# Reordering the steps of the first layer's context attention and feed-forward: probability transposes later, down products in halves, normalizations emitted later

## The chip, the cores and the metric

One core of a Trainium2 chip runs the whole kernel. The metric is the device time in microseconds; lower is better. The time before is the median of 3 runs, 3416.09 us (3408.83 to 3417.53).

Engine names in the profile: PE is TensorE (PEld its weight loads), DVE is VectorE, ACT is ScalarE, POOL is GpSimd, SP is SyncE, which issues DMAs. Each engine works through its own queue in the order in which the program was built.

## The reference, cut to what matters

Two decoder layers on x of shape (8, 512, 256), with layer normalization after each of three sublayers. The change touches the second and third sublayer of the first layer:

```python
x = _layernorm(x + _L0_attn_ref(x, ...))
x = _layernorm(x + _L0_xattn_ref(x, ctx, ctx, mask))   # 16 heads of 16, 64 context keys, no projections
x = _layernorm(x + _L0_ffn_ref(x, ...))                # 256 -> 1024, gelu, 1024 -> 256, biases
x = _layernorm(x + _L1_attn_ref(x, ...))
...
```

`_L0_xattn_ref` masks and scales `q k^T`, takes a softmax over 64 keys and multiplies with the values. In `_L0_ffn_ref` the butterfly stages were folded into the two weight matrices earlier in the kernel.

## The kernel before, in words

The kernel runs stage after stage: the first layer's self-attention, then the stage of this change (context attention and feed-forward of layer 0, in one interleaved loop), then layer 1. x stays on chip as eight tiles `xs[b]`, one per batch element ("batch" below), each as 4 blocks of 128 rows.

The loop of the stage is near line 895: `for n in range(len(steps_) + 3)`, with `b, i = n // 4, n % 4`. A step is one block of 128 rows of one batch. PE is scheduled by hand here (`tc.manual_schedule(engines={PE})`): its queue has exactly the order of the calls. The queues of DVE, ACT and POOL are ordered by the scheduler of the language when the program is built, and fixed from then on; a call given to `tc.keep_in_program_order` is held to its place in the text.

The pieces of a step, in the order of before:

- `l0x_keys` (at i=0, line 699), for the next batch: two products on POOL that spread the context over heads (`bd`, L703), the mask's DMA (L710), and its bias on DVE (L712).
- `l0x_scores` (line 715): score matmuls into two PSUM tiles (`s_xs`, L725); DVE adds the mask bias and so empties PSUM (L735), takes the maximum (L741); POOL subtracts it (L742); ACT takes the exponential (L743); DVE sums (L744). The result `p` is used one step later.
- `l0x_transposes` (line 747) of the step before: PE turns the probabilities (`tP`, L755), ACT copies them to `pt` (L756).
- one piece `up` of the feed-forward (line 818): eight passes of 512 columns into `s_h` (L823), two gelus on ACT (L832). Exponential and gelu need different ACT tables, so each step loads two.
- `l0x_values` at i=0 (line 758): value products `s_xpv` (L764) from `pt`; ACT copies them to `oT` (L773); DMAs of a later batch's context values on SP (L780).
- `l0x_back` at i=1 (line 785): PE turns `oT` back (`tO`, L800), DVE divides by the sums (L802), POOL adds the residual (L808), `normed` follows.
- at i=2, `turned_x` of the next batch: PE turns x (`tT`, L695), ACT copies it to `xT` (L696).
- one piece `down` (line 834): 8 matmuls of one row block (`o_out`, L846). After two blocks DVE adds `xb`, which is x plus biases, made on POOL (L837), into `r` (L856); after the fourth, `normed`.
- at i=2, `ffn(b - 1)` (line 813): turns the normalized x once more and queues four `up` pieces and four `down` pieces.

`normed` (line 206): DVE statistics (L213, L214), plus epsilon (L215); POOL's power (`rs`, L216); DVE's shift (L220); then four scalings on ACT (L224) that write `xs[b]`. With `then` given, the last part (from L220) is not emitted but appended to a list.

The feed-forward lags: `ffn(b - 1)` is called at step i=2 of batch b, its `up` pieces run in the next four steps, its `down` pieces in the four after those. While a `down` list is empty, `one` takes a piece from `early` instead: the unfinished output of the self-attention and four transposes of the second matrix (`wdn_piece`).

PSUM: two buffers for `s` tiles (`s_xs` twice, `s_h`, and `s_xpv` share them), three banks for `t` tiles (`tP`, `tO`, `tT`, and the second half of a `down` result), one for `o` (its first half). A tile's buffer is written again once its last reader is done.

Of the kernel before, what the change touches and what calls it, by code (L numbers as in the profile page):

```python
# [11 lines left out]
F32 = mybir.dt.float32  # L12
I32 = mybir.dt.int32
AF = mybir.ActivationFunctionType
ALU = mybir.AluOpType
# [3 lines left out]
P = 128  # L19
S = 512  # L20
D = 256
S2 = 64
NT = S // P
# [26 lines left out]
def decoder_kernel(ctx: ExitStack, tc: tile.TileContext, a: dict, out: bass.AP):  # L50
    nc = tc.nc
    NB = a["x"].shape[0]
# [10 lines left out]
    pe, act, dve, pool, sp = nc.tensor, nc.scalar, nc.vector, nc.gpsimd, nc.sync  # L63
# [3 lines left out]
    work = ctx.enter_context(tc.tile_pool(name="work", bufs=2))  # L67
# [49 lines left out]
    one = const.tile([1, 1], F32, name="one")  # L117
# [11 lines left out]
    xs = [const.tile([P, NT, D], F32, name=f"x{b}") for b in range(NB)]  # L129
# [47 lines left out]
    dnb = const.tile([P, D], F32, name="dnb")  # L177
# [28 lines left out]
    def normed(dst, r, on_act=False, then=None):  # L206

        st = work.tile([P, NT, 6], F32, tag="st", name="st")
        mv = work.tile([P, NT, 2], F32, tag="mv", name="mv")
        ve = work.tile([P, NT], F32, tag="ve", name="ve")  # L210
        rs = work.tile([P, NT], F32, tag="rs", name="rs")
        for i in range(NT):
            dve.bn_stats(st[:, i, :], r[:, i, :])  # L213
            dve.bn_aggr(mv[:, i, :], st[:, i, :])  # L214
        dve.tensor_scalar(ve, mv[:, :, 1], LN_EPS, None, ALU.add)  # L215
        pool.tensor_tensor(rs, ve, mhalf, ALU.pow)  # L216

        def scaling(held=lambda instruction: instruction):
            if on_act:
                dve.scalar_tensor_tensor(ve, mv[:, :, 0], -1.0, rs, ALU.mult, ALU.mult)  # L220
            for i in range(NT):
                if on_act:
                    held(
                        act.activation(dst[:, i, :], r[:, i, :], AF.Identity, bias=ve[:, i : i + 1], scale=rs[:, i : i + 1])  # L224
                    )
                    continue
                dve.tensor_scalar(
                    dst[:, i, :], r[:, i, :], mv[:, i, 0:1], rs[:, i : i + 1], ALU.subtract, ALU.mult
                )

        if then is None:
            scaling()
        else:
            then.append(scaling)

    def r_tile():
        return work.tile([P, NT, D], F32, tag="r", name="r", bufs=1)
# [547 lines left out]
    def l0x_back(b):  # L785

        oT, sums = live.pop(("oT", b)), live.pop(("sums", b))
        rsum = ph.tile([P, NT, 16], F32, tag="rsum16", name="rsum16")
        for i in range(NT):
            dve.reciprocal(  # L790
                rsum[:, i, :].rearrange("p (c r e) -> p c r e", c=KC, r=4),
                sums[:, i, :].rearrange("p (r c e) -> p c r e", c=KC, r=4),
            )
        rx = ph.tile([P, NT, D], F32, tag="rx", name="rx", bufs=1)
        for i2 in range(2):
            t = t_tile("tO")
            for j in range(2):
                i = 2 * i2 + j
                for c in range(KC):
                    pe.transpose(t[:, 2 * j + c, :], oT[:, c, i * P : (i + 1) * P], ident)  # L800
            two = slice(2 * i2, 2 * i2 + 2)
            dve.tensor_tensor(  # L802
                rx[:, two, :].rearrange("p i (h n) -> p (i h) n", n=16),
                t.rearrange("p i (h n) -> p (i h) n", n=16),
                rsum[:, two, :].rearrange("p i h -> p (i h)").unsqueeze(2).to_broadcast([P, 32, 16]),
                ALU.mult,
            )
            pool.tensor_tensor(rx[:, two, :], rx[:, two, :], xs[b][:, two, :], ALU.add)  # L808
        normed(xs[b], rx, on_act=True)

    ups, downs = [], []

    def ffn(b):
        xT = turned_x(b)
        gs = gates[b % 2]
        made = {}

        def up(f2):
            s = s_tile("s_h")
            for j in range(2):  # L820
                f = 2 * f2 + j
                for c in range(KC):
                    pe.matmul(  # L823
                        s[:, j, :],
                        lhsT=wup[:, c, f * P : (f + 1) * P],
                        rhs=xT[:, c, :],
                        start=(c == 0),
                        stop=(c == KC - 1),
                    )
            for j in range(2):  # L830
                f = 2 * f2 + j
                act.activation(gs[f], s[:, j, :], AF.Gelu, bias=upb[:, f : f + 1])  # L832

        def down(i):
            if i == 0:
                xb = work.tile([P, NT, D], F32, tag="att", name="xb")
                pool.tensor_tensor(xb, xs[b], dnb.unsqueeze(1).to_broadcast([P, NT, D]), ALU.add)  # L837
                made["xb"], made["r"] = xb, r_tile()
            xb, r = made["xb"], made["r"]
            i2, j = i // 2, i % 2  # L840
            if j == 0:
                made["o"] = (t_tile("o_out").rearrange("p i n -> p (i n)") if i2 else o_tile("o_out")).rearrange(
                    "p (i n) -> p i n", i=2
                )
            for f in range(8):
                pe.matmul(  # L846
                    made["o"][:, j, :],
                    lhsT=gs[f][:, i * P : (i + 1) * P],
                    rhs=wdn[:, f, :],
                    start=(f == 0),  # L850
                    stop=(f == 7),
                )
            if j == 0:
                return
            two = slice(2 * i2, 2 * i2 + 2)
            dve.tensor_tensor(r[:, two, :], made["o"], xb[:, two, :], ALU.add)  # L856
            if i2 == 1:
                normed(xs[b], r, on_act=True)

        ups.extend(partial(up, f2) for f2 in range(4))  # L860
        waiting.append([partial(down, i) for i in range(NT)])

    waiting = []

    with phase("l0_context_ffn") as ph, tc.manual_schedule(engines={PE}):
        v2 = [ph.tile([P, 8, 32], F32, name=f"v2{n}", bufs=1) for n in range(2)]
        for n in range(2):
            pool.memset(v2[n], 0.0)
            l0x_context(n)
        l0x_keys(0)  # L870
        live["xT", 0] = turned_x(0)
        more = [slot(f"gate{n}") for n in range(2)]
        few = ph.tile([P, 8, S], F32, name="few", bufs=1)
        gates = [
            [few[:, f, :] for f in range(8)],
            [more[f // 4][:, f % 4 * S : (f % 4 + 1) * S] for f in range(8)],
        ]
        weights_of_layer_1()
        wdn = ph.tile([P, 8, D], F32, tag="wdn", name="wdn", bufs=1)

        def wdn_piece(f):
            t = t_tile("tW")
            for j in range(4):
                pe.transpose(t[:, j, :], wdnT[:, j % 2, (f + j // 2) * P : (f + j // 2 + 1) * P], ident)
            act.copy(wdn[:, f : f + 2, :].rearrange("p f n -> p (f n)"), t.rearrange("p j n -> p (j n)"))

        steps_ = [(b, i) for b in range(NB) for i in range(NT)]
        early = unfinished + [partial(wdn_piece, f) for f in range(0, 8, 2)]

        def one(queue):  # L890
            if queue:
                queue.pop(0)()
            elif early:
                early.pop(0)()

        for n in range(len(steps_) + 3):
            b, i = n // NT, n % NT
            if i == 0 and b + 1 < NB:
                l0x_keys(b + 1)
            if n < len(steps_):  # L900
                l0x_scores(b, i)
            if 0 < n <= len(steps_):
                l0x_transposes(*steps_[n - 1])
            one(ups)
            if i == 0 and b:
                l0x_values(b - 1)
            if i == 1 and b:
                l0x_back(b - 1)
            if i == 2 and b + 1 < NB:
                live["xT", b + 1] = turned_x(b + 1)  # L910
            if i == 3 and waiting and len(waiting) > 1 or (i == 3 and waiting and not ups):
                downs.extend(waiting.pop(0))
            one(downs)
            if i == 2 and b:
                ffn(b - 1)
        while ups or downs or waiting:
            if ups:
                ups.pop(0)()
            if not downs and waiting and (len(waiting) > 1 or not ups):
                downs.extend(waiting.pop(0))  # L920
            if downs:
                downs.pop(0)()

    turned = slot("turned").rearrange("p (two j n) -> p two j n", two=2, j=2)
    woT1 = slot("woT1").rearrange("p (c n) -> p c n", c=8)
# [808 lines left out]
```

## Time and profile before

| | us |
|---|---|
| median of the 3 runs | 3416.09 |
| lowest, highest | 3408.83, 3417.53 |
| the profiled execution, own time | 3412.61 |
| its span, first to last instruction | 3410.9 |
| mean granted TensorE clock | 0.974 |
| stage of the change: first `s_xs` to the next layer | 778.8 to 1184.4 |
| first `s_xs` of steps 7, 11, 15, 19, 23, 27, 31 (i=3) | 826.09, 866.21, 908.29, 957.43, 1005.91, 1055.73, 1102.94 |

Busy time of PE in the span is 3217.6 us. The page has one digit per 85 us; a row of digits shows tenths of busy time. In a line of the timeline the columns are start, duration (both us), engine, line, operation, output<-input, shape, count, and in brackets the idle time of that engine just before, with what ended it. A line of waits names who waited for what, then total us, times, and the longest.

### The profile page before, as it was taken

How to read it: one execution, taken by the hardware profiler on the slowest of the kernel's cores; microseconds unless marked ns; L12 is line 12 of the kernel's file. 1: busy time of each engine (PE TensorE's matmuls, PEld its weight loads, DVE VectorE, ACT ScalarE, POOL GpSimd, SP SyncE). 2: the span in 40 equal slices, each digit the busy share in tenths (PEclk: the TensorE clock that was granted, in tenths of full speed). 3: DMA queues.
4: the chain of work that ended last, by engine and by line, in shares of the span. 5: the costliest groups of instructions: out<-in, count | busy, mean ns of one | idle time of the engine just before them, and what ended most of it. 6: DMA issues, size and time to landing. Idle time of an engine off the chain costs nothing. (4 is left out here: it accounts for less than half of the span.)

```text
span 3410.9 us, 53375 instructions
## 1 busy us (share of the span) xinstructions
PE 3217.6 (94%) x19638; PEld 2030.8 (60%) x19638; DVE 1992.7 (58%) x6491; ACT 1590.2 (47%) x3280; POOL 1122.8 (33%) x1049
## 2 busy tenths in 40 slices
PE   7999999997888989999999999999999999999995
PEld 3444444445555656766666665555555557888884
DVE  5777777765455277787777865666776664100102
ACT  2444454455666355565556653444444443222222
POOL 3777777764333122222222210011111111222222
PEclk8999999998999999999999999999999999999997
DMA  4000011110000099323333320000000006666674
GB/s 138 26 26 29 29 32 44 40 52 12 18 2 1 27 254 240 44 38 38 41 40 43 42 44 4 10 14 23 20 20 18 14 18 205 186 187 185 186 231 136
DMA packets 166006, 235.00 MB, mean 69 GB/s; under 512 B 26569, under 2 KB 128649, under 8 KB 165746
## 3 DMA queue, kind: packets, MB, share of 16 engines
q1 hardware_dynamic: 139010, 175.83, 16.3%
q0 software_dynamic: 25584, 51.57, 10.7%
q10 hardware_dynamic: 1152, 4.19, 0.3%
q8 instruction: 155, 2.54, 0.3%
q14 instruction: 105, 0.86, 0.1%
HBM read 135.83 MB, written 61.11 MB: 58 GB/s over the span
## 5 line engine op out<-in xcount | busy, mean ns | idle before, releaser
L438 DVE CUSTOM_DVE_ANT_0 scored<-s_sc,decay 128x512 f32<-128x512 f32 x512 | 332.5, 687 | 191.0 <-PE s_sc L433 191.0
L290 ACT ACTIVATE p<-p,nm 128x384 f32<-128x384 f32 (+3 forms) x512 | 282.4, 552 | 256.0 <-DVE nm L279 256.0
L979 POOL DMA_DIRECT2D qk<-turned x256 | 203.7, 1222 | 579.2 <-PE s_sc L1019 300.0
L496 ACT ACTIVATE pt<-s_st 128x1024 f32<-128x1024 f32 x256 | 261.8, 1024 | 268.5 <-PE s_st L492 242.1
L1004 DVE TENSOR_SCALAR p<-p,rsum 128x576 f32<-128x576 f32 (+4 forms) x768 | 300.8, 434 | 10.2
L1223 ACT ACTIVATE p<-s_sc,nm 128x576 f32<-128x576 f32 x256 | 189.4, 742 | 195.5 <-DVE nm L1222 173.8
L1590 DVE TENSOR_SCALAR y<-o_y,share 128x256 f32<-128x256 f32 x71 | 34.3, 484 | 403.5 <-PE o_y L1570 403.5
L1553 PE MATMUL s_h<-xnT,we 128*128 128x256 f32 (+1 forms) x1248 | 258.8, 361 | 0.0
L1570 PE MATMUL o_y<-we,h 128*128 128x256 f32 x1136 | 251.4, 379 | 0.0
L279 DVE CUSTOM_DVE_ANT_0 p<-s_sc,tabs 128x384 f32<-128x384 f32 (+3 forms) x512 | 225.1, 484 | 44.7 <-PE s_sc L1019 42.4
L1591 POOL DMA_INDIRECT total<-y,to x71 | 110.2, 1552 | 385.9 <-DVE y L1590 198.7
L1570 PEld LDWEIGHTS o_y<-we,h 128*128 128x128 f32 x1136 | 215.3, 190 | 29.0
L1553 PEld LDWEIGHTS s_h<-xnT,we 128*128 128x128 f32 x1248 | 215.4, 190 | 23.9 <-ACT xnT L1532 0.2
L1222 DVE TENSOR_REDUCE nm<-s_sc 128x1 f32<-128x576 f32 x256 | 183.3, 749 | 77.2 <-PE s_sc L1218 76.1
L1052 ACT COPY pt<-tP 128x384 f32<-128x384 f32 (+1 forms) x384 | 167.0, 527 | 56.2 <-PE tP L1051 56.0
L1019 PE MATMUL s_sc<-qk 64*128 64x384 f32 (+3 forms) x1024 | 178.6, 462 | 14.7 <-DMA qk<-turned 9.5
L1051 PEld LDWEIGHTS tP<-ident,p 128*128 128x128 f32 x1280 | 141.3, 141 | 51.7 <-issue 30.5
L1218 PE MATMUL s_sc<-k,q 64*128 64x288 f32 x1024 | 166.3, 437 | 3.3 <-ACT p L1223 3.1
L1051 PE MATMUL tP<-ident,p 128*128 128x128 f32 x1280 | 163.1, 278 | 3.2 <-ACT pt L1052 2.2
L433 PE MATMUL s_sc<-k,q 32*128 32x512 f32 x1024 | 154.5, 647 | 3.2 <-ACT k L418 1.7
L450 DVE TENSOR_SCALAR_CACHE_REDUCE diag<-scored,mx 128x128 f32<-128x128 f32 x512 | 155.7, 342 | 0.0
L1074 PE MATMUL o_pv<-pt,vc 128*64 128x128 f32 (+1 forms) x2304 | 154.5, 288 | 0.0
(290 smaller groups left out, 6322.7 us busy)
## 6 DMA issues: line engine op xcount, KB each, us to landing
we<-in_mo_w SPq DMA_DIRECT2D x78, 1024.0 KB
rows_in<-zero SPq DMA_DIRECT2D x64, 530.0 KB
qk<-turned POOLq DMA_DIRECT2D x256, 128.0 KB, 4.6
coef<-in_ff_upw SPq DMA_DIRECT2D x40, 256.0 KB
coef<-in_ff_dnw SPq DMA_DIRECT2D x40, 256.0 KB
xr<-rows_in SPq DMA_DIRECT2D x32, 265.0 KB
x<-in_x SPq DMA_DIRECT2D x8, 512.0 KB
total<-x SPq DMA_DIRECT2D x8, 512.0 KB
```

Of the source, the lines that this page charges most:

```text
L279: dve.tensor_tensor_reduce(out=p[:, j, 0:n], in0=s[:, j, 0:n], in1=m, scale=-scale, scalar=3.0e38, op0=ALU.add, op1=ALU.min, accum_out=nm[ ...
L290: act.activation(p[:, j, 0:n], p[:, j, 0:n], AF.Exp, bias=nm[:, j : j + 1], scale=-1.0, accum_out=sums[:, at + j : at + j + 1],)
L438: dve.tensor_tensor_reduce(out=scored[:, h, :], in0=s[:, j, :], in1=decay[:, i, :], scale=1.0, scalar=-3.0e38, op0=ALU.mult, op1=ALU.max, ...
L496: tc.keep_in_program_order(act.activation(pt, s, AF.Exp, scale=1.0 / 16.0))
L979: pool.dma_start(out=qk[h : h + 32], in_=other[g : g + 32], accum_op=ALU.add)
L1004: dve.tensor_scalar(p[:, j, 0:n], p[:, j, 0:n], rsum[:, j : j + 1], None, ALU.mult)
L1019: pe.matmul(s[:, j, at : at + n], lhsT=q[h : h + 64, i * P : (i + 1) * P], rhs=k[h : h + 64, 0:n], start=True, stop=True,)
L1051: pe.transpose(t[:, n, :], p[:, j, at * P : (at + 1) * P], ident)
L1222: dve.tensor_reduce(nm[:, j : j + 1], s, AX.XY, ALU.max, negate=True)
L1223: act.activation(p[:, j, :].rearrange("p (t n) -> p t n", t=2), s, AF.Exp, bias=nm[:, j : j + 1], accum_out=sums[:, j : j + 1])
L1553: pe.matmul(s[:, j, :], lhsT=w1[:, c, f * P : (f + 1) * P], rhs=xnT[:, c, :], start=(c == 0), stop=(c == KC - 1),)
L1570: pe.matmul(o, lhsT=h[:, f, i * P : (i + 1) * P], rhs=w2[:, f, :], start=(f == 0), stop=(f == 7),)
```

## The change

The order of PE's calls in a step becomes: scores; half a `down` piece; `up`; the scaling part of a finished feed-forward normalization, if any; transposes of the step before; then by i the values, the way back, or the scaling part of the context normalization and `turned_x`; keys of the next batch (at i=0, now after the values); another half `down` piece; `ffn`. A `down` list has eight pieces of 4 matmuls in place of four of 8. The two scaling parts are held in program order. POOL's residual add moves to DVE. `xb` is made in `ffn`, not with the first `down` piece.

```diff
-            pool.tensor_tensor(rx[:, two, :], rx[:, two, :], xs[b][:, two, :], ALU.add)
-        normed(xs[b], rx, on_act=True)
+            dve.tensor_tensor(rx[:, two, :], rx[:, two, :], xs[b][:, two, :], ALU.add)
+        normed(xs[b], rx, on_act=True, then=backs)
...
-    ups, downs = [], []
+    ups, downs, backs, ends = [], [], [], []
...
         made = {}
+        xb = work.tile([P, NT, D], F32, tag="att", name="xb")
+        pool.tensor_tensor(xb, xs[b], dnb.unsqueeze(1).to_broadcast([P, NT, D]), ALU.add)
...
-        def down(i):
-            if i == 0:
-                xb = work.tile([P, NT, D], F32, tag="att", name="xb")
-                pool.tensor_tensor(xb, xs[b], dnb.unsqueeze(1).to_broadcast([P, NT, D]), ALU.add)
-                made["xb"], made["r"] = xb, r_tile()
-            xb, r = made["xb"], made["r"]
+        def down(n):
+            if n == 0:
+                made["r"] = r_tile()
+            r = made["r"]
+            i, half = n // 2, n % 2
             i2, j = i // 2, i % 2
-            if j == 0:
+            if j == 0 and half == 0:
...
-            for f in range(8):
+            for f in range(4 * half, 4 * half + 4):
...
-            if j == 0:
+            if j == 0 or half == 0:
                 return
...
-                normed(xs[b], r, on_act=True)
+                normed(xs[b], r, on_act=True, then=ends)
...
-        waiting.append([partial(down, i) for i in range(NT)])
+        waiting.append([partial(down, n) for n in range(2 * NT)])
...
+        def scale(queue):
+            if queue:
+                queue.pop(0)(tc.keep_in_program_order)
+
         for n in range(len(steps_) + 3):
             b, i = n // NT, n % NT
-            if i == 0 and b + 1 < NB:
-                l0x_keys(b + 1)
             if n < len(steps_):
                 l0x_scores(b, i)
+            if i == 3 and waiting and (len(waiting) > 1 or not ups):
+                downs.extend(waiting.pop(0))
+            one(downs)
+            one(ups)
+            scale(ends)
             if 0 < n <= len(steps_):
                 l0x_transposes(*steps_[n - 1])
-            one(ups)
             if i == 0 and b:
                 l0x_values(b - 1)
             if i == 1 and b:
                 l0x_back(b - 1)
+            if i == 2 and b:
+                scale(backs)
             if i == 2 and b + 1 < NB:
                 live["xT", b + 1] = turned_x(b + 1)
-            if i == 3 and waiting and len(waiting) > 1 or (i == 3 and waiting and not ups):
-                downs.extend(waiting.pop(0))
-            one(downs)
+            if i == 0 and b + 1 < NB:
+                l0x_keys(b + 1)
+            if downs:
+                downs.pop(0)()
             if i == 2 and b:
                 ffn(b - 1)
...
-            if downs:
-                downs.pop(0)()
+            for _ in range(2):
+                if downs:
+                    downs.pop(0)()
+                scale(ends)
+        scale(ends)
```

## Prediction, on record before the changed kernel ran

> **What bounds the kernel now.** I read the page first. TensorE (PE) is busy 94% of the span, so a change pays only where PE stands still or runs slow.
>
> ```profile
> PE 3217.6 (94%) x19638; PEld 2030.8 (60%) x19638; DVE 1992.7 (58%) x6491; ACT 1590.2 (47%) x3280; POOL 1122.8 (33%) x1049
> PE   7999999997888989999999999999999999999995
> PEclk8999999998999999999999999999999999999997
> ```
>
> A slice is 85 us. The changed stage begins at 778.8 us (first `s_xs`) and ends at 1184.4, when the next layer takes over: the 10th to 14th digits of the PE row (7, 8, 8, 8, 9). The stretches, cut at the score matmuls of step i=3 of each batch, give the room:
>
> ```profile
> core 0: us, PE busy (x) PEld busy (x) DVE busy (x) ACT busy (x) POOL busy (x), PEclk, DMA share, GB/s
> 957.43:1005.91 48.48, 41.26 (x233) 27.11 (x233) 24.55 (x46) 30.74 (x42) 16.51 (x12) 0.93 0.02 2
> ```
>
> 48.48 us per batch, with 7 us of idle PE. Other engines are half busy, so what counts is who waits for whom. The waits of the stage:
>
> ```profile
> PEld tP L755 <- ACT xT L696: 22.7, 4, 5.9
> PEld tP L755 <- ACT p L743: 12.5, 4, 4.4
> PEld s_h L823 <- DVE p L735: 11.7, 6, 3.0
> ```
>
> The first line is one stall of 5.7 us per steady batch: a probability transpose waits for a PSUM bank, whose copy stands on ACT behind a feed-forward normalization. The second lies in the first steps only. In the third PE waits 1.5 us a batch until DVE has emptied the score bank. Everything the change can remove is in these three, plus slow clock after the stalls. Now ACT in one ordinary step, whose scores started at 924.91:
>
> ```profile
> 926.27 1.07 ACT L756 COPY pt<-tP 128x512 f32<-128x512 f32 x2 [3.44 <-PE tP L755]
> 927.36 1.28 ACT L743 ACT_TABLE_LOAD   x1
> 930.32 1.06 ACT L743 ACTIVATE p<-p 128x1024 f32<-128x1024 f32 x1 [1.68 <-POOL p L742]
> 931.39 1.28 ACT L832 ACT_TABLE_LOAD   x1
> 932.69 1.26 ACT L832 ACTIVATE few<-s_h,upb 128x512 f32<-128x512 f32 x2
> 933.84 1.07 ACT L773 COPY oT<-s_xpv 128x512 f32<-128x512 f32 x2
> ```
>
> The `pt` copies are ACT's first work of the step (at +1.36). The exponential cannot start before +5.41, since scores, DVE's add (1.29), maximum (1.22) and POOL's subtraction (1.90) precede it; the table switch and the gelus end at +9.04. This chain is the same in every undisturbed step.
>
> **The change part by part.** I compared both built programs engine by engine, with the semaphore of each wait.
>
> *Unchanged amounts.* The halves are the same 256 second-matrix matmuls (8 pieces of 4 per batch for 4 of 8). Table loads stay two a step. PE work of a batch, from start-to-start times of the timeline: per step scores .65, `tP` .87, up 3.45, down 3.46 (two halves of 1.73), so 33.7; plus `s_xpv` 1.86, `tO` .87, two `tT` 1.74: 38.2 us.
>
> *Residual add on DVE.* 2 per batch go from POOL (row L808: 1.27 each) to DVE. The nearest DVE row of that size is L856, 0.69: 1.4 us more DVE per batch, on the way to the next step's L735. The chain from `tO` to that L735 becomes 1.29+1.38+2.0 (statistics, as in the trace) = 4.7, about as before; cost 0 either way.
>
> *Keys later.* The mask DMA now passes behind the two context DMAs on SP, needed a batch later; two `bd` products (1.04 each) keep their place in POOL's queue, ahead of the step's subtraction, and L712 its place on DVE. `xb`, issued earlier, still waits for the last L856, whose buffer it reuses. All 0: cover is four steps; without it the price would be the 2 us of `bd`.
>
> *Deferred feed-forward normalization.* On ACT its four scalings (2.07) go behind the four `xT` copies and that step's gelus. The 5.65 us stall goes. But DVE's part stays ahead of the next scores in DVE's queue: from L856's end to the next L735 the trace has 957.05 to 961.69, 4.64 us, through POOL's `xb` and `rs`. It is next late.
>
> *Probabilities turned later.* Here is the price. In the new ACT order each step reads: exponential, table load, gelus, then the `pt` copies. Their matmuls end at +6.7, but the copies now wait for the gelus, so they land at about +9.6 and +10.1, where they landed at +1.9 and +2.4. Three consumers follow `tP` at once: in step i=0 `s_xpv` reads `pt`; in i=1 both `tO`, in i=2 the first `tT`, need the banks that the two `tP` hold, because the second output bank of the down product, now allocated at the first half-piece of i=1, keeps the third bank. Each of these waits names that step's `pt` copy in the new program. Behind them in PE's queue stand the down half and the next scores.
>
> *The sum for a steady batch.* Time 0 is the end of the last `pt` copy of i=2. Scalings to 2.07, first two `xT` copies to 3.15; the last `tT` ends at 3.65, scores of i=3 start. The down half before it ended at 2.2, L857 at 3.15, so L735 starts at 7.8 (+4.64) and `up` at 8.5, not 6.05. `tP` and down end 14.6. Gelus of i=3: L735 9.1, maximum 10.3, POOL 12.35, exp 13.45, end 16.0; so the second score bank of i=0 (start 14.6) is written from 16.0, scores end 16.5. Chain again: gelus end 24.85, first copy 25.4; `s_xpv` waits for it from 22.6, down half ends 29.1. Step i=1: start 29.1, `tP` ends 35.8, first copy 38.7, `tO` to 39.7, down half 41.4. Step i=2: DVE reaches L735 at 44.1; maximum 47.3, POOL 49.3, exp 50.4, gelus 52.95, copies 54.05; `tT` has waited from 49.1 to 53.5. Period 54.05 against 48.48.
>
> *All batches.* Before, steps 15-18, 19-22, 23-26 took 49.14, 48.48, 49.82: +4.9, +5.6, +4.2. Steps 27-30 took 47.21; the last batch turns no next x, so about 51.3: +4. Steps 11-14 took 42.08; no feed-forward normalization precedes, 3.4 us less than the period, 50.65: +8.6. Steps 7-10 took 40.12; same walk without down pieces gives 49: +9. Steps 0-6: two exponential waits (2.84 and 3.70) lose up to 4.6 to early pieces that now stand ahead: -3. The tail (81.5 us, PE 78.4 busy) has no scores left: 0. Sum +33.
>
> *Clock.* Idle PE per batch grows from 7 to 15.7 us, in gaps of 2.4, 2.8, 2.9 and 4.4. What follows a gap:
>
> ```profile
> 948.29 3.70 PE L823 MATMUL s_h<-xT,wup 128*128 128x512 f32 x8 [1.52 <-DVE p L735]
> ...
> 1107.41 5.40 PE L823 MATMUL s_h<-xT,wup 128*128 128x512 f32 x8 [2.72 <-DVE p L735]
> ```
>
> The same eight matmuls take 3.70 after 1.5 us of idling and 5.40 after 2.7. [...] The trace comes first, but the other two gaps near 2.5 us (ends at 854.4, 865.2) were followed by losses of 1.4 and 0.6 only, so I take 2.5 for five batches and 1 for steps 7-10: 13.5. Ends: 0 and 21.
>
> Forecast: +33 +13.5 = +47. The profiled execution took 3412.6 (span 3410.9), so 3460; it was 3.5 below the median of the runs (3416.1), so a median of 3463.
>
> **The rivals.** *Faster (0.11).* If copies of `pt` don't gate PE, each steady batch comes down to 38.2 of work plus about 2 of waiting for gelus and DVE: some 8 us for four batches, plus 3 at the start, 35 in all: 3381. It decides by when the exponential ends: at +4.1 instead of +6.5 the copies would meet `tP`. The trace speaks against it: +5.41 is its start in every undisturbed step, with DVE and POOL idle ahead of it.
>
> *Awash (0.08).* The stalls are those of the walk, but early steps gain more, clock costs nothing, and waits overlap: within 10 us of 3416. For it: my +33 has 9 and 8.6 from batches whose walk rests on few rows.
>
> *Slower without clock loss* is inside my case: 3449. With a full loss and longer DVE queueing it is 3475 to 3485.
>
> **How the numbers follow.** Slower by queueing on ACT 0.81, faster 0.11, no change 0.08; a measurement here tells 0.3% (10 us) from no change. Likeliest 3463. The range leaves out the faster case and a little of each end: 3420 to 3488.
>
> **What would show it.** In the new profile: the 5.7 us wait of `tP` on `xT` gone; new waits of `s_xpv`, `tO` and `tT` on ACT `pt` of near 3, 3 and 4 us a batch; `pt` copies directly after the gelus; steps of 12 to 13 us where they were 9.5 and 10.6; period 54 to 57; nothing changed before 778 or after the stage. I am wrong if those waits are under 1 us (then faster), or if DVE's L735 sits ahead of the deferred chain.

## The result, and the profile after

The changed kernel takes 3474.78 us (median of 4 runs, 3467.53 to 3481.33); the kernel before, run beside it, 3416.81. The ratio is 1.0172, 95% interval 1.0144 to 1.0200: 58 us slower, where +47 was forecast. The profiled execution took 3473.05 us, span 3471.1, mean clock 0.967.

The page of the changed kernel, engine totals and the two PE rows:

```profile
PE 3248.7 (94%) x19638; PEld 2040.7 (59%) x19638; DVE 2001.2 (58%) x6507; ACT 1587.8 (46%) x3280; POOL 1104.0 (32%) x1033
...
PE   7999999997878989999999999999999999999995
...
PEclk8999999997888999999999999999999999999998
```

The same 19638 matmuls keep PE busy 31 us longer: those us are the same work done more slowly, and the clock row shows where: digits 10 to 13 (7, 8, 8, 8), the slices of the stage, which were 8, 9, 9, 9 before. In the stage PE was busy for 88.3 us at a granted clock of 0.50, against 50.4 before; half of the difference, some 19 us, is an estimate of what the lower clock cost. Outside the stage little moved. Taken from its first score matmul to the first matmul of the next stage (`o_lat`), the stage took 406.1 us before (778.80 to 1184.93) and takes 461.6 now (780.76 to 1242.35): +55.5 of the span's +60.2. Outside the stage the profiled executions of all kernels here range from 2997 to 3016 us, though no edit lies there, so below I give each kernel's stage length in its profiled execution beside the median.

| steps | before | after | change | forecast with clock |
|---|---|---|---|---|
| 0-6 | 47.29 | 48.49 | +1.2 | -3 |
| 7-10 | 40.12 | 47.70 | +7.6 | +10 |
| 11-14 | 42.08 | 55.00 | +12.9 | +11.1 |
| 15-18 | 49.14 | 58.09 | +9.0 | +7.4 |
| 19-22 | 48.48 | 58.05 | +9.6 | +8.1 |
| 23-26 | 49.82 | 58.03 | +8.2 | +6.7 |
| 27-30 | 47.21 | 54.93 | +7.7 | +6.5 |
| the tail | | | -0.7 | 0 |

One steady batch of the changed kernel, steps 19 to 22, engine by engine (columns: stretch, its length, busy time and instructions of PE, PEld, DVE, ACT, POOL, granted clock, DMA share and GB/s):

```profile
990.04:1048.09 58.05, 46.28 (x233) 29.50 (x233) 25.75 (x48) 30.41 (x42) 13.99 (x9) 0.88 0.01 2
```

Before, the batch was 48.48 with PE busy 41.26. Subtract busy from length in both: idle PE grew from 7.22 to 11.77, by 4.55, and the same 233 records of matmuls took 5.02 longer. The loss is about half waiting, half slower running.

The five longest waits of PE's matmuls in the stage of the changed kernel:

```profile
PE s_xpv L764 <- ACT pt L756: 17.4, 7, 3.5
PE tT L695 <- ACT pt L756: 16.2, 5, 3.8
PE s_h L825 <- DVE p L735: 14.7, 8, 2.8
PE tO L800 <- ACT pt L756: 13.1, 5, 2.6
PE tP L755 <- ACT p L743: 9.5, 4, 4.5
```

The stall of `tP` on `xT` (22.7 us before) is gone. In its place stand three waits for the same instruction, the copy `pt`, and a longer one for DVE's addition. The timeline shows how the first of them comes about, and the others behind it:

```profile
1008.72 1.06 ACT L743 ACTIVATE p<-p 128x1024 f32<-128x1024 f32 x1 [1.72 <-POOL p L742]
1009.79 1.28 ACT L834 ACT_TABLE_LOAD   x1
1011.09 1.26 ACT L834 ACTIVATE gate<-s_h,upb 128x512 f32<-128x512 f32 x2
1012.24 1.07 ACT L756 COPY pt<-tP 128x512 f32<-128x512 f32 x2
1012.88 3.89 PE L764 MATMUL s_xpv<-pt,v 128*32 128x512 f32 x16 [2.59 <-ACT pt L756]
...
1028.19 1.14 PE L800 MATMUL tO<-ident,oT 128*128 128x128 f32 x8 [2.61 <-ACT pt L756]
...
1041.93 1.97 PE L695 MATMUL tT<-ident,x 128*128 128x128 f32 x8 [3.82 <-ACT pt L756]
1043.69 3.60 PE L847 MATMUL o_out<-wdn,few 128*128 128x256 f32 x8
...
1053.50 5.37 PE L825 MATMUL s_h<-xT,wup 128*128 128x512 f32 x8 [2.76 <-DVE p L735]
```

The step's scores began at 1003.33. ACT waits for POOL, takes the exponential, switches tables, does the gelus, and only then copies: at 1012.24, 8.9 us into the step. The transposes themselves began at 1009.25 and take 1.04. Read the second column too: `s_xpv` takes 3.89 where undisturbed it takes 1.92, the `up` matmuls 5.37 for 3.60, the down half 3.60 for 1.89.

### The profile page after: what moved, and what is told of

The parts are those of the page before. It is cut to its first block, busy times and chain, and to the rows that moved or that the text cites. A ratio compares the mean times of both kernels' runs of the same rounds, so it can differ in the third digit from the quotient of the medians.

```text
span 3471.1 us, 53386 instructions
## 1 busy us (share of the span) xinstructions
PE 3248.7 (94%) x19638; PEld 2040.7 (59%) x19638; DVE 2001.2 (58%) x6507; ACT 1587.8 (46%) x3280; POOL 1104.0 (32%) x1033
```

## The experiments

My theory: moving the transposes behind the `up` piece costs more than the whole loss; the rest of the change gains. What it costs comes in two parts of like size, PE standing still for the copies, and PE running slower after it stood. Rivals: the loss comes from the rest (the halves, the deferral, DVE's added work), or the waits are all of it and the clock only follows the chip. All kernels, with their ratio to runs of before made with them:

| kernel | median us | ratio, 95% interval | stage us |
|---|---|---|---|
| before | 3416.81 | | 406.1 |
| changed | 3474.78 | 1.0172 (1.0144 to 1.0200) | 461.6 |
| changed, transposes early | 3400.27 | 0.9948 (0.9932 to 0.9965) | 395.1 |
| before, transposes late | 3494.59 | 1.0221 (1.0204 to 1.0238) | 484.6 |
| changed, `pt` copied by DVE | 3417.39 | 1.0002 (0.9989 to 1.0014) | 409.6 |
| changed, one gap filled | 3455.88 | 1.0111 (1.0094 to 1.0128) | 452.3 |
| before, deferral alone | 3408.26 | 0.9971 (0.9958 to 0.9984) | 396.1 |
| before, halves alone | 3415.92 | 0.9989 (0.9977 to 1.0000) | 404.0 |
| transposes early, addition on POOL | 3407.28 | 0.9972 (0.9962 to 0.9982) | 395.5 |
| transposes early, scaling ahead of exp | 3399.11 | 0.9944 (0.9928 to 0.9960) | 390.1 |
| the same, `xb` later | 3384.50 | 0.9907 (0.9890 to 0.9924) | 382.2 |
| the same, x turned early | 3391.11 | 0.9937 (0.9914 to 0.9960) | 382.5 |
| changed, `xb` later | 3455.22 | 1.0122 (1.0103 to 1.0141) | 447.5 |

### The changed kernel with the transposes early again

```diff
                 l0x_scores(b, i)
+            if 0 < n <= len(steps_):
+                l0x_transposes(*steps_[n - 1])
...
             scale(ends)
-            if 0 < n <= len(steps_):
-                l0x_transposes(*steps_[n - 1])
```

> The changed kernel, with the probability transposes back directly behind the scores; halves, deferred normalizations, residual add on DVE stay. Queue theory (the copies of the turned probabilities stand behind the gelus on ACT, and PE waits for them): the waits of s_xpv, tO and tT on those copies fall from about 9 us a batch to under 1, the 5.7 us stall of before does not come back, the period of four steps is 43 to 46 us (58.1 after, 48.5 before), and the kernel takes 3385 to 3405 us. Rival (the deferred normalizations, the DVE residual add or the halves carry the loss): the period stays above 54 us and the time above 3455.

Measured 3400.27. A steady batch of it, and the waits of its stage:

```profile
959.47:1002.74 43.27, 40.92 (x234) 26.70 (x233) 23.28 (x47) 30.53 (x42) 14.45 (x10) 0.98 0.02 2
```

```profile
PE tT L695 <- ACT x L224: 17.7, 24, 2.6
...
PE tP L755 <- ACT p L743: 12.0, 4, 4.5
...
PE s_xpv L764 <- ACT pt L756: 0.6, 1, 0.6
```

The three waits for `pt` are gone, down to 0.6 us in all. PE idles 2.35 us a batch and the clock is at 0.98. Moving one call back removes the whole loss, and what is left of the change gains 16 us. The largest wait left is for the scalings of x, deferred behind the gelus.

### The kernel before with only the transposes late

```diff
-            if 0 < n <= len(steps_):
-                l0x_transposes(*steps_[n - 1])
             one(ups)
+            if 0 < n <= len(steps_):
+                l0x_transposes(*steps_[n - 1])
```

> The kernel before, with one edit: the probability transposes stand behind the up piece instead of ahead of it. Queue theory: ACT copies them behind the gelus, s_xpv waits 2 to 4 us for them in each step i=0 and tO up to 3 us in i=1, the 5.7 us stall of step i=3 stays in some form, and the time is 3450 to 3480. Rival (other parts carry the loss): within 10 us of 3417.

Measured 3494.59, 78 us above before and 15 above the top of what was expected. A batch, and the waits:

```profile
994.76:1059.59 64.83, 47.12 (x234) 30.86 (x233) 24.63 (x46) 30.74 (x42) 16.53 (x11) 0.87 0.01 2
```

```profile
PE s_h L823 <- ACT xT L696: 25.5, 5, 6.5
PE s_xpv L764 <- ACT pt L756: 21.0, 8, 3.5
PE tT L695 <- ACT pt L756: 16.1, 5, 3.5
```

The old stall behind the normalization stays (now `s_h` waits 6.5 us for `xT`) and the waits for `pt` are added. Moving the one line costs +78 us from before and +75 from the changed kernel with the transposes early; in stages +78.5 and +66.5. That the old stall, which grows from 5.7 to 6.5 beside the late transposes, makes it dearer is likely but was not tested alone. The rest of the change is worth 16 us with the transposes early and 20 with them late.

### The copies of `pt` on DVE

The row sums follow the copies, so that they don't stand ahead of them in DVE's queue.

```diff
-        dve.tensor_reduce(live["sums", b][:, i, :], p, AX.X, ALU.add)
...
-            act.copy(pt[:, 4 * c : 4 * c + 4, i * P : (i + 1) * P], t)
+            tc.keep_in_program_order(dve.tensor_copy(pt[:, 4 * c : 4 * c + 4, i * P : (i + 1) * P], t))
+        tc.keep_in_program_order(dve.tensor_reduce(live["sums", b][:, i, :], p, AX.X, ALU.add))
```

> The changed kernel with the same order on PE, but DVE in place of ACT copies the turned probabilities, in program order, with the row sums of a step taken one step later so that they don't stand ahead of the copies on DVE. Queue theory: the copies land 1 us behind the transposes, the waits of s_xpv, tO and tT on them go below 0.7 us each, the period is 43 to 47 us and the time 3385 to 3410. Rival (the place in PE's order itself costs, whoever copies): the waits stay, and the time is above 3455. DVE gets 1.4 us more work a step.

Measured 3417.39, 7 us above the range expected: 57 us come back with the transposes left where the change put them. With the transposes early it was 74.5, so ACT's queue makes most of the price, and the late place with DVE copying still costs 17 us (in stages 52.0 of 66.5 come back). A batch and one of the three places:

```profile
966.93:1013.60 46.67, 42.41 (x234) 26.79 (x233) 30.16 (x55) 26.58 (x34) 13.96 (x10) 1.00 0.02 2
```

```profile
984.03 1.29 DVE L756 COPY pt<-tP 128x512 f32<-128x512 f32 x2 [3.43 <-PE tP L755]
984.78 2.51 PE L765 MATMUL s_xpv<-pt,v 128*32 128x512 f32 x16 [0.35 <-DVE pt L756]
```

PE still waits, 0.35 us at each of the three consumers, and `s_xpv` takes 2.51 for 1.92 at a clock of 1.00, most likely at the pace of the second copy. No wait of this batch is over 0.88 us. The batch has the length expected; steps 0 to 6 are longer than in any other kernel here, 51.4 us (48.5 in the changed one), and why was not followed up.

### One gap filled with matmuls that nobody reads

Three more matmuls (six passes) write the tile of `s_xpv` just before the real ones overwrite it.

```diff
+        for _ in range(3):
+            pe.matmul(s[:, 0, :], lhsT=wup[:, 0, 0:P], rhs=wup[:, 0, 0:S], start=True, stop=True)
```

> The changed kernel with three needless 128x512 matmuls into the value tile ahead of s_xpv, 2.6 us of PE work that is overwritten, where PE now waits 2.6 us for the copy. If a wait of 2.6 us costs PE its full clock, s_xpv falls from 3.9 us to about 2.0 and the kernel gets about 1.9 us faster in each of seven batches: 13 us, 3462. If a gap that short leaves the clock alone, s_xpv stays at 3.9 and the time at 3475, or longer if the filler is in the way.

Measured 3455.88, 19 us less than the changed kernel although it does more, and 6 less than the clock's theory expected.

```profile
1003.58 2.74 PE L763 MATMUL s_xpv<-wup 128*128 128x512 f32 x6
...
1006.33 2.40 PE L766 MATMUL s_xpv<-pt,v 128*32 128x512 f32 x16
```

`s_xpv` begins as late as before in its step (9.55 us after the scores) but takes 2.40 for 3.89. That 1.5 us is slow running and nothing else. The batch is 56.55 at clock 0.91, and the stage 9.3 us shorter: 1.1 to 1.7 in each of six steps i=0, and little else in sum. In three batches the step i=2 fell from 17.1 to between 14.4 and 15.2 with no edit there, but the step i=1 ahead of it rose from 12.4 to between 13.7 and 14.1. The profiled execution was the slowest of its four (3461.47); what the medians show beyond the stage's 9.3 us is in no trace.

### The deferral alone, and the halves alone

The first is the kernel before with both normalizations given `then=` and their scalings called behind `one(ups)`, held in program order; the second is the kernel before with eight half pieces of `down`, one ahead of `up` and one at the step's end.

```diff
-        normed(xs[b], rx, on_act=True)
+        normed(xs[b], rx, on_act=True, then=backs)
...
-                normed(xs[b], r, on_act=True)
+                normed(xs[b], r, on_act=True, then=ends)
...
             one(ups)
+            scale(ends)
+            if i == 2 and b:
+                scale(backs)
```

> The kernel before with only the normalizations' scaling deferred (both of them called behind the up-projection piece and held in program order); transposes early, pieces whole. In the before trace the scaling stands ahead of the copies on ACT and TensorE's longest gap of a batch (5.65 us, the second half of the transposes in the step i=3) follows it. If that gap is what the rest of the change removes, this alone gives most of the 16 us that the change gave with the transposes early: 3395 to 3408 us. Rival: the halves of the second matrix give it; then this stays at 3412 to 3420.

```diff
-            for f in range(8):
+            for f in range(4 * half, 4 * half + 4):
...
+            one(downs)
             one(ups)
```

> The kernel before with only the second matrix in halves, one half ahead of the up-projection piece and one at the step's end; normalizations as before, transposes early. If the deferral is what removes the 5.65 us gap, this is within 3408 to 3422 us. Rival: the halves, standing between the scores and what reads them, give the 16 us: 3398 to 3406 us.

Measured 3408.26 for the deferral, 0.3 us above what was expected, and 3415.92 for the halves. In stages: -10.0 and -2.2, beside -11.1 for both together with the rest. The deferral is what gains. In its own waits (first fence) the stall of `tP` on `xT` no longer appears among the large ones, and in the kernel with halves alone (second fence) it does:

```profile
PE s_h L823 <- DVE p L735: 16.3, 10, 2.1
...
PE tP L755 <- ACT p L743: 11.5, 4, 4.2
PE tT L695 <- ACT x L224: 8.5, 7, 4.1
```

```profile
PE tP L755 <- ACT xT L696: 12.2, 4, 4.0
```

Deferral turns a stall of 5.7 us into one of 2.1 for DVE's L735, as the prediction's "it is next late" had it.

### The addition back on POOL

The kernel with the transposes early, and `pool.tensor_tensor` in place of `dve.tensor_tensor` at L808.

> The run with the transposes early (3400 us) with the addition of x behind the turned context (two instructions a batch, 0.64 us each on DVE) back on POOL, where each took 1.26 us. In the seventh step of the stage, where the change lost 3.1 us instead of gaining, the addition stood on DVE between the products and the statistics; if that is why, this gains 1 to 3 us there: 3396 to 3400 us. Rival: the step was lost to the scaling split in two around the exponential on ACT, and POOL's longer addition delays the shift of the scores: 3401 to 3408 us.

Measured 3407.28, which missed the expectation and lies in the rival's range. But the stage is 395.5 against 395.1: the addition's place is worth nothing in the stage, and the difference of the two kernels lies outside it, where no edit was. What the run does settle is step 6, which takes 12.93 before, 16.05 in the changed kernel and with the transposes early, 14.75 here and 14.75 with the deferral alone. So of 3.1 us lost there 1.3 came with the addition on DVE and 1.8 with the deferral.

### The scaling ahead of the exponential, then `xb` later, then x turned early

Three steps, each on the one before, starting from the kernel with the transposes early.

```diff
+            if i == 2 and b:
+                scale(backs)
             if n < len(steps_):
                 l0x_scores(b, i)
```

> The run with the transposes early (3400 us) with the context normalization's scaling called ahead of the step's scores, so that ACT does it before the exponential instead of behind the gelus. In that run's trace the scaling's inputs are ready 5.7 us before ACT reaches it, and TensorE waits 1.7 to 2.6 us for it at the turn of x in each steady batch and runs slower behind it. Expected: these waits gone in 6 batches and some of the clock with them, 3382 to 3392 us. Rival: the exponential is then late instead and its readers wait, 3398 to 3405 us.

```diff
-        xb = work.tile([P, NT, D], F32, tag="att", name="xb")
-        pool.tensor_tensor(xb, xs[b], dnb.unsqueeze(1).to_broadcast([P, NT, D]), ALU.add)
         def up(f2):
+            if f2 == 1:
+                made["xb"] = work.tile([P, NT, D], F32, tag="att", name="xb")
+                tc.keep_in_program_order(
+                    pool.tensor_tensor(made["xb"], xs[b], dnb.unsqueeze(1).to_broadcast([P, NT, D]), ALU.add)
+                )
```

> The run with the transposes early and the scaling ahead of the exponential (3399 us) with POOL's xb issued in the second up-projection piece, held there, instead of at the feed-forward's start. In that run POOL works on xb (2.37 us) just when DVE's two small instructions of the normalization stand between the last sum of a batch and the next score addition (L215 1.50 and L220 1.00 us, 0.16 each elsewhere), and rs waits for xb. Expected: the chain from that sum to the next score addition falls from 5.3 to about 3 us, the wait of the scores in the first step of a batch (1.4 us) goes: 6 batches, 3386 to 3394 us. Rival: those scores wait for the gelus anyway: 3396 to 3402.

```diff
             one(downs)
+            if i == 2 and b + 1 < NB:
+                live["xT", b + 1] = turned_x(b + 1)
             one(ups)
```

> As the run before, and the next x is turned ahead of the up-projection piece, so that ACT copies it before the gelus; TensorE waited 2.9 us a batch for these copies. Expected: 3 us and some clock in 6 batches, 3365 to 3382 us. Rival: the turn now waits for the scaling of x on ACT, and the up-projection behind it: 3390 to 3405 us.

Measured 3399.11, 3384.50 and 3391.11. The first missed its expectation and lies in its rival's range. The wait on `x` fell from 17.7 us to 2.0, and the copies of `xT`, which the scheduler left behind the gelus, are late in its place (its waits):

```profile
PE tT L695 <- ACT xT L696: 14.6, 5, 2.9
```

The second did a little more than it should, 15 us in the medians and 7.9 in the stage, and is the fastest kernel here: 0.9907 of before. The third missed its expectation and lies in its rival's range. It takes the wait for `xT` away (13.4 us in the second, 2.8 left) and gives it back at once, because the second score tile of the next step then waits for the gelus to empty a buffer (5.7 us in the second):

```profile
PE s_xs L725 <- ACT few L837: 11.4, 7, 2.8
```

Stages of 382.2 and 382.5 say that this exchange is even.

### The changed kernel with `xb` later

The edit of the second step above, made on the changed kernel, nothing else.

> The changed kernel (3475 us) with POOL's xb issued in the second up-projection piece, nothing else. The prediction counted 2.4 us a batch and some clock for the wait of the up-projection in step i=3 on DVE's score addition, behind a chain of 4.64 us through xb and rs. If the chain is held by xb, it falls to about 2.5 us, the wait of 2.7 goes and the slow matmuls behind it (1.8 us) too: 4 to 5 batches, 3455 to 3465 us. Rival: the step is held by the gelus behind it and the gain is given back in the next step: 3470 to 3477 us.

Measured 3455.22, at the low edge of what was expected. First the chain of the changed kernel in step i=3, from a batch's last statistics to the score addition, then the same in this kernel:

```profile
1048.16 2.37 POOL L818 TENSOR_TENSOR xb<-x,dnb 128x1024 f32<-128x1024 f32 x1 [10.43 <-DVE r L857]
...
1049.05 1.50 DVE L215 TENSOR_SCALAR ve<-mv 128x4 f32<-128x4 f32 x1
...
1050.70 1.02 POOL L216 TENSOR_TENSOR rs<-ve,mhalf 128x4 f32<-128x4 f32 x1 [0.17 <-DVE ve L215]
...
1052.67 1.27 DVE L735 TENSOR_TENSOR p<-s_xs,bias 128x512 f32<-128x512 f32 x2
```

```profile
983.45 0.17 DVE L215 TENSOR_SCALAR ve<-mv 128x4 f32<-128x4 f32 x1
...
983.76 1.01 POOL L216 TENSOR_TENSOR rs<-ve,mhalf 128x4 f32<-128x4 f32 x1 [11.66 <-DVE ve L215]
...
985.72 1.27 DVE L735 TENSOR_TENSOR p<-s_xs,bias 128x512 f32<-128x512 f32 x2
986.54 1.53 PE L828 MATMUL s_h<-xT,wup 128*128 128x512 f32 x3 [1.01 <-DVE p L735]
```

From L215's start to L735 it was 3.62 us, and is 2.27; the wait of `up` falls from 2.76 to 1.01. The batch shows what that is worth:

```profile
982.88:1037.52 54.64, 43.99 (x234) 29.06 (x233) 24.43 (x48) 30.41 (x42) 13.96 (x9) 0.94 0.02 2
```

Of the 3.4 us that the batch gained, 1.1 is idle PE (11.77 to 10.65) and 2.3 is faster running (46.28 to 43.99). `up` takes 3.67 for 5.37. `s_xpv` takes 2.40 for 3.89 too, although its own wait hardly changed (2.44 for 2.59); the section on gaps below has a likely reason. So the shorter wait mattered more for the clock than for itself.

## Why the prediction was right

**The mechanism held.** Three waits for `pt` of "near 3, 3 and 4 us" were named; they are 2.59, 2.61 and 3.82. The wait of `up` in i=3 on L735, "next late" after 4.64 us, is there with 2.76; the chain took 4.66. The stall on `xT` is gone. Putting the line back and moving it alone show that the late transposes make the whole loss; taking the copies off ACT shows that at least 57 of the 74.5 us that they cost come from ACT's queue.

**The clock was mis-sized, and the waiting the other way.** The forecast for a steady batch was 56.55: 54.05 by the walk and 2.5 for the clock. The waits in the walk add up to 13.75 (`up` 2.45, the second score tile 1.25, `s_xpv` 2.8, `tO` 2.9, `tT` 4.4), which leaves 40.3 of work. Measured are 58.05, just above the "54 to 57" named: 11.77 of idle PE and 46.28 of busy PE, of which 12.03 passed at a granted clock of 0.50. The 128x512 matmuls of `up` start 0.85 us apart at 0.50 and 0.43 apart at 1.00, in this trace and in the one of before. At that half speed the 12.03 cost an estimated 6.0, which leaves 40.3 of work. No run shows the 2.5 us a batch that the forecast has for the clock, nor the 21 us of its upper end; the 6.0 a batch stand in their place. So the walk had the work right (its listed sum of 38.2 is 2.1 short: a down half behind the scores takes 1.83 from start to start, not 1.73, and a transpose with a wait behind it 1.04, not 0.87), the clock was 3.5 too small, and the waiting 2.0 too large. That the two errors left only 1.5 a batch is luck.

The clock error is in the step *Clock*. The slow running after a gap is visible four times a batch: `up` 5.37 for 3.60, `s_xpv` 3.89 for 1.92, the first `tT` 1.97 for 1.04, the down half behind it 3.60 for 1.89, together 6.4. I set aside the row with 5.40 after a gap of 2.72 because two other gaps had cost less; here it came closer. The largest part of the other error follows from it. The walk had the scores of i=0 wait 1.25 for the gelus. In the changed kernel they don't: `up` ran so slowly that the gelus were done at 1002.78, before these scores began (1003.33). With `xb` later, where `up` runs at full speed, that wait is there, with 0.78.

**Where the gaps fell.** The trace has losses after gaps of 2.59, 2.74 and 3.82. But length alone does not tell them: 2.61 ahead of `tO` was followed by a down half of 1.89, full speed. In the traces of before and of the changed kernel the granted clock of the stage is 1.00 or 0.50, and its changes (21 before, 42 after) all lie whole multiples of 3.41 us apart. Two gaps of the changed kernel, in stretches of 3.41 us between such points:

```profile
992.52:995.93 3.41, 0.67 (x2) 0.30 (x2) 2.21 (x4) 0.71 (x1) 3.03 (x3) 1.00 0.00 0
995.93:999.35 3.42, 3.42 (x6) 1.33 (x5) 1.41 (x2) 0.20 (x1) 1.90 (x1) 0.50 0.00 0
...
1023.24:1026.65 3.41, 2.34 (x12) 1.32 (x10) 1.47 (x2) 2.59 (x3) 0.76 (x1) 1.00 0.00 0
1026.65:1030.07 3.42, 1.88 (x13) 1.71 (x14) 1.18 (x2) 3.26 (x5) 0.00 (x0) 1.00 0.00 0
1030.07:1033.48 3.41, 3.41 (x29) 2.52 (x27) 3.41 (x12) 0.00 (x0) 0.00 (x0) 1.00 0.00 0
```

The gap of 2.74 ahead of `up` lies in one stretch, where PE is busy for 0.67 us only, and the next stretch runs at half the clock. The gap of 2.61 ahead of `tO` is shared by two stretches with 2.34 and 1.88 of busy PE, and nothing follows. Counted over the stage in these two traces, a stretch at full clock with more than 2.0 us of idle PE was followed by one at half the clock 25 times out of 25; with less than 1.0 us never in 154; in between 5 times in 26 (after 1.13, 1.62, 1.76, 1.91 and 1.93 us, but not after 1.72 and 1.88). The same wait of the same length in the kernel with the filled gap shows both outcomes:

```profile
965.47 1.97 PE L802 MATMUL tO<-ident,oT 128*128 128x128 f32 x8 [2.61 <-ACT pt L756]
...
1020.15 1.14 PE L802 MATMUL tO<-ident,oT 128*128 128x128 f32 x8 [2.61 <-ACT pt L756]
```

In the first, 2.02 us of the gap lie in one stretch, in the second 1.95. By this reading, filling one gap moved a loss from the step i=2 to i=1, and `s_xpv` kept its speed with `xb` later (2.40), because its gap of 2.44 is shared 1.90 and 0.53 there. The three batches of 58.03 to 58.09 are 17 of these stretches (58.03) long, and the half clock comes back at the same places: from 982.28, 995.93 and 1013.00 in one batch, from 1040.31, 1053.96 and 1071.03 in the next.

**The early steps.** "-3" for steps 0 to 6 came as +1.2. Steps 0 to 5 did gain, 34.36 to 32.44, most in step 1 (10.14 to 6.87); step 6 lost 3.1. I had put the addition on DVE at 0, by the chain of a later batch, and had no term for the deferral there. They cost 1.3 and 1.8 in that step. A likely reason is that no `up` piece runs yet in this step, so nothing stands on PE while DVE and ACT finish x; in a steady batch such a piece does.

**Batches.** Steps 7 to 10 lost 2.4 less than forecast, the later ones 1.2 to 1.8 more; only the batch of steps 19 to 22 was taken apart, above. The tail was put at 0, and -0.7 was measured.

## What to carry to other kernels

Look at what stands ahead of a copy in its engine's queue, not at when its input is ready: behind exponential, table switch and gelus copies of 0.5 us each held up three consumers a batch. If a walk uses undisturbed durations, all slow running of the new period has to be added to it, not only what is new: the period before held 3.11 us of busy PE at half the clock already. Ask of a gap not only how long it is, but where it falls: here 2.74 us within one stretch were followed by half the clock, 2.61 shared by two were not. And when a wait is removed, name the next instruction in the same queue before counting the gain; twice here the gain was handed on within a step.

## What was not expected of the hardware

Two small DVE instructions took longer beside some of POOL's. In the changed kernel's batch L215 (128x4) takes 1.50 us while POOL works on `xb` and, with `xb` later, 0.17 when `xb` is elsewhere; L220 takes 1.00 beside `bd` and, in the fastest kernel, 0.16 ahead of it:

```profile
998.09 1.01 POOL L216 TENSOR_TENSOR rs<-ve,mhalf 128x4 f32<-128x4 f32 x1 [4.71 <-DVE ve L215]
...
999.13 0.16 DVE L220 SCALAR_TENSOR_TENSOR ve<-mv,rs 128x4 f32<-128x4 f32 x1 [1.19 <-POOL rs L216]
...
1000.13 2.05 POOL L703 TENSOR_TENSOR bd<-ctxT,small 128x512 f32<-128x512 f32 x2 [1.03 <-PE s_xs L725]
```

In the changed kernel's batch L215 ends at 1050.55, 0.02 us after `xb` (1050.53), and L220 (start 1051.75, 1.00 us) at 1052.75, 0.02 us after the first of the two `bd` products (start 1051.69, 1.04 each). In the tail L215 began 0.16 us after an `xb`, took 2.21 us and again ended 0.03 us behind it. The three ends look like being held until POOL's instruction is over, rather than slowed. Not every DVE instruction was: in the same batch L213 took 0.41 beside `xb` and L735 0.68 beside the second `bd` product, and in the whole stage neither took over 0.43 and 0.69.

And the kernel with three more matmuls per batch was 19 us faster in the medians than without them, 9.3 in its stage.
